# A branch taken out of the last row block, and a sort cut into three pieces between hop products

## The chip, the cores and the metric

One core of one Trainium2 chip runs the kernel. The metric is device microseconds of one execution, as the median of several runs. "PE" is TensorE's matmul, "PEld" its weight load, DVE is VectorE, ACT ScalarE, POOL GpSimd, SP SyncE, which here issues most of the DMAs.

## The reference

Two graph layers over 4096 nodes with 256 features, each as x = x + layer(relu(layernorm(x))). Layer 0 is a graph attention with four heads over the given adjacency. Layer 1 is a diffusion of two steps, and the change lies in it. Cut to what matters:

```python
def _top_p_attention(X, W1, W2, W3):
    q = X @ W1.T @ W2.T
    k = X @ W3.T
    probs = softmax(q @ k.T, axis=-1)
    idx = argsort(-probs, axis=-1)
    sp = take_along_axis(probs, idx, axis=-1)
    cs = cumsum(sp, axis=-1)
    keep_sorted = cs - sp < 0.9          # the fewest largest that reach 0.9
    A = probs * (the mask keep_sorted, put back by idx)
    return A / A.sum(-1, keepdims=True)

R = S + eye(N);  R = R / R.sum(-1, keepdims=True)     # S is the adjacency
for n in range(2):
    A = _top_p_attention(Xa, W1, W2, W3)
    Xf = R @ Xf
    Xa = A @ Xa
    Z = Z + Xf @ U1[n].T + Xa @ U2[n].T
out = layernorm(X + Z) * ln_g + ln_b
```

## The kernel before

The rows are 32 blocks of 128. After layer 0 (until about 822 us) each of the two steps has two stages.

**The hop** is R @ Xf, 4 passes over 8 row blocks each, 32 source blocks in a pass: 128 pairs of a source block and a pass. `hops` is a generator that yields twice in a pair, after each half of its eight products (L577). For pair m an adjacency tile of 512 KB is loaded (`edge`, L547, into four buffers "ar" and one "aru"), in step 1 also a source tile "x" or "xa" of 128 KB (`source`, L537, five buffers); in step 0 the sources lie on the chip. The source is split into a high part (ACT, L554) and a rest (DVE, L555), "hl", five buffers: `split(A, n)`, some four pairs ahead of the products. Where the pair lies on the diagonal (8 pairs in each pass, 80 to 87 in the third), DVE adds the identity to the tile: `own(A, m + 3)`, L564, the "own row". The products of pair m need its tile, its own row and both parts of hl.

**Beside the hop** two more generators are advanced between the halves of the pairs. `fills` makes the projections and the logits of the first three row blocks, their exponentials and first probes. `picks` finds the threshold of these three blocks and masks them, all on DVE: two halves of a probe (L899), `searching`, two halves of the mask (L899). `searching` takes the 8 largest of each of 18 segments (L923, three groups of six, a yield behind each), sorts the 48 largest out of the 144 (L930 and L932, six rounds), yields, and finds the threshold by a running sum (L934 to L941, "the scan group"). In `picks` each yield of `searching` becomes four steps:

```python
            for _ in searching(r, found):
                yield from waits(3)
```

The orders of PE, DVE, ACT, POOL and SP are written out by hand (`manual_schedule`): an instruction stands in its engine's queue where the Python code records it.

**The row blocks** follow, one `attend` for each of the 32: eight groups of four transposes (L1010), ACT's copy of them ("eT", L1012) and eight products (L1018) with the features. `between[g]` puts other work behind group g. For all but the first three blocks the threshold is found here, in `chosen_kept`, by the same `searching` run through at once (`candidates`).

Rows whose 48 candidates don't decide the threshold are counted: `questioned`, `counted`, `chosen`. Blocks with such rows are computed again behind the step: `prepared` makes the exponentials anew, searches by bisection and handles ties (its products are L1134, its exponentials L1139), `completed` redoes the products and writes the rows. In the kernel before, the first such block is prepared inside the last row block, behind its group 0, under a branch on the count that all engines have loaded into a register (L1101):

```python
            def beginning():
                finish(blocks[NB - 2])
                R.count = number(R, R.undone)
                with tc.If(R.count > 0):
                    prepared(R)
```

`finish` adds up block 30's result on DVE. The branch itself, and what each engine does where the body is skipped, have the line L1309. The second branch, in `repaired` (L1178), stands behind the step and holds `completed` and a loop over further blocks. Group 2 of the last block starts hop 2's first loads in step 0 (`begin`: four tiles and four sources), groups 5 and 6 split them; behind the last block PE makes the first halves of hop 2's products.

Of the kernel before, what the change touches and what calls it, by code (L numbers as in the profile page):

```python
# [56 lines left out]
def gat_then_top_p_diffusion(  # L57
# [738 lines left out]
    def table(name):  # L796
        return small.tile([P, NB], F32, name=name, bufs=1)

    def col(name, bufs=None):
        return small.tile([P, 1], F32, name=name, bufs=bufs or 4)  # L800
# [112 lines left out]
    def searching(r, found):  # L913

        t, after, eighth = (x[:, r.b:r.b + 1] for x in found)
        seg = SEG
        cand = small.tile([P, SEG, 8], F32, name="cand", bufs=2)
        best = small.tile([P, CAND], F32, name="best", bufs=2)

        cum = small.tile([P, CAND + 1], F32, name="cum", bufs=2)  # L920
        edges = [N * s // seg for s in range(seg + 1)]
        for s in range(seg):
            nc.vector.max(cand[:, s, :], big[:, edges[s]:edges[s + 1]])  # L923
            if s % 6 == 5:
                yield
        nc.vector.tensor_scalar(cum[:, :1], r.z, 1.0 - TOP_P, r.low3, ALU.mult, ALU.subtract)
        nc.vector.tensor_reduce(eighth, cand[:, :, 7], AX.X, ALU.max)
        flat = cand.rearrange("p s k -> p (s k)")
        for i in range(CAND // 8):
            nc.vector.max(best[:, ts(i, 8)], flat)  # L930
            if i + 1 < CAND // 8:
                nc.vector.match_replace(flat, best[:, ts(i, 8)], flat, -1.0)  # L932
        yield
        nc.vector.tensor_tensor_scan(cum[:, 1:], best, zero.to_broadcast([P, CAND]), cum[:, :1], ALU.add, ALU.add)  # L934

        drop = small.tile([P, CAND], F32, name="drop", bufs=2)
        work = small.tile([P, CAND], F32, name="work", bufs=2)
        nc.vector.tensor_scalar(drop, cum[:, :CAND], 0.0, 3.0e38, ALU.is_ge, ALU.mult)
        nc.vector.tensor_tensor_reduce(work, drop, best, 1.0, best[:, :1], ALU.add, ALU.min, t)
        nc.vector.tensor_scalar(work, drop, -1.0, 3.0e38, ALU.mult, ALU.add)  # L940
        nc.vector.tensor_tensor_reduce(work, best, work, 1.0, -3.0e38, ALU.subtract, ALU.max, after)  # L941
        r.t = t
# [55 lines left out]
    def loads(r):  # L998
        r.xf, r.part = rows.tile([P, KC, P], F32, name="xf"), rows.tile([P, D], F32, name="part", bufs=3)
        nc.sync.dma_start(r.xf, xft_d[r.n][ds(r.b, 1)].rearrange("o p s i -> (o p) s i"))  # L1000
        if r.n > 0:
            nc.sync.dma_start(r.part, block(z_d, r.b))
            r.x1 = rows.tile([P, D], F32, name="x1", bufs=3)
            nc.sync.dma_start(r.x1, block(x1_d, r.b))
        r.acc = ps1.tile([P, 2, D], F32, name="acc")
# [111 lines left out]
    def index(R, engine):  # L1117
        return nc.values_load(R.ids_i[:, :1], engines=[engine], min_val=0, max_val=NB - 1)
# [34 lines left out]
    def completed(R, cur):  # L1153

        r = SimpleNamespace(n=R.n, b=index(R, ET.SP), e=R.e, scale=R.scale)
        dve = index(R, ET.DVE)
        loads(r)
        r.ri = col("a_ri", 1)
        nc.vector.tensor_copy(r.ri, rinv[:, ds(dve, 1)])
        if r.n + 1 < STEPS:  # L1160
            r.x = rows.tile([P, D], F32, name="a_x", tag="xa")
            nc.vector.tensor_copy(r.x, X[:, ds(dve, 1), :].rearrange("p o d -> p (o d)"))
        eT = [turn(r, 0)]
        for g in range(NB // 4):
            if g + 1 < NB // 4:
                eT.append(turn(r, g + 1))
            gather(r, eT[g], g, cur)
        scaled(r)
        contributed(r, contribute(r))
        finish(r)  # L1170
        finish_scale(r)
        finish_rows(r)
        rest = small.tile([1, NB], I32, name="a_rest", bufs=1)
        nc.vector.tensor_copy(rest[:, 1:], R.ids_i[:, 1:])
        nc.vector.tensor_copy(R.ids_i[:, :NB - 1], rest[:, 1:])

    def repaired(R, cur):
        with tc.If(R.count > 0):  # L1178
            completed(R, cur)
            with tc.For_i(0, nc.values_load(R.rest_i, engines=everyone, min_val=0, max_val=NB), 1):  # L1180
                prepared(R)
                completed(R, cur)
# [70 lines left out]
    for n in range(STEPS):  # L1253
        cur = X
        G = SimpleNamespace()
        found = [table(f"found{i}") for i in range(3)]
        blocks = {}
        with tc.manual_schedule(engines=every):
            pieces = first_hop if n == 0 else hops(second)
            filling, picking = fills(n, G, found, blocks), picks(n, found, blocks)  # L1260
            done = 0 if n else NB - G0 - LOOK
            for i, _ in enumerate(pieces, 2 * done):
                if n > 0 and i % 6 == 5 and i // 6 < NB // 4:
                    g = i // 6
                    nc.sync.dma_start(cur[:, ts(g, 4), :], xa_d[ts(g, 4)].rearrange("b p d -> p b d"))
                if (n == 0 or i > 10) and i // 2 % NB != NB - 2:
                    next(filling, None)
                    if i // 2 % NB < NB - 3 or i % (2 * NB) == 2 * NB - 1:
                        next(picking, None)
                if i == 2 * len(order) - 6:  # L1270
                    first = turn(blocks[0], 0)
            weights(n)
            for _ in filling:
                next(picking, None)
            for _ in picking:
                pass

            def chosen_kept(b):

                r = blocks[b]  # L1280
                if not hasattr(r, "kept"):
                    candidates(r, found)
                if b > 2:
                    finish_scale(blocks[b - 3])
                if b + 2 < NB and not hasattr(blocks[b + 2], "stepped"):
                    first_step(blocks[b + 2])
                if b + 1 < NB and not hasattr(blocks[b + 1], "thirded"):
                    third_probe(blocks[b + 1])
                if b > 1:
                    finish(blocks[b - 2])  # L1290
                if b > 2:
                    finish_rows(blocks.pop(b - 3))
                if not hasattr(r, "kept"):
                    masked(r)

            R = SimpleNamespace(n=n, kT=G.kT, qT=G.qT, nm=G.nm, table=found[0])

            def last_chosen():
                chosen_kept(NB - 1)
                R.failed, R.undone = questioned(G, found)  # L1300

            def looked():
                counted(R)
                chosen(R)

            def beginning():
                finish(blocks[NB - 2])
                R.count = number(R, R.undone)
                with tc.If(R.count > 0):  # L1309
                    prepared(R)  # L1310

            beside = {NB - 2: {5: last_chosen, 6: looked}, 0: dict(zip((0, 1, 3, 5, 6), S.turned))}
            for b in range(NB - 1):
                chosen_kept(b)
                if b + AHEAD < NB:
                    blocks[b + AHEAD] = began(n, b + AHEAD, G)
                attend(blocks[b], cur, blocks.get(b - 1), blocks.get(b + AHEAD),
                       beside.get(b, {}), [first] if b == 0 else ())
            r = blocks[NB - 1]

            def earlier():
                for b in range(NB - 3, NB - 1):
                    finish_scale(blocks[b])
                for b in range(NB - 3, NB - 1):
                    finish_rows(blocks[b])

            beside = {0: beginning, 3: earlier}
            if n + 1 < STEPS:
                second = hop_of(n + 1)
                beside.update({2: lambda: begin(second, 4), 5: lambda: split(second, 2), 6: lambda: (split(second, 4), own(second, 4))})  # L1330
            attend(r, cur, blocks[NB - 2], None, beside)
            contributed(r, contribute(r))
            for m in range(second.begun if n + 1 < STEPS else 0):
                for s in range(KC):
                    graph_products(second, m, s, (0,))
            finish(r)
            finish_scale(r)
            finish_rows(r)
        repaired(R, cur)


# [30 lines left out]
```

## Time and profile before

| | |
|---|---|
| median of 3 runs | 2939.87 us (2936.16, 2939.87, 2939.92) |
| profiled execution | 2939.0 us, span 2937.2 us |
| busy: PE, PEld | 2832.3 us (96%), 2476.5 us (84%) |
| busy: DVE, ACT, POOL | 2197.3 us (75%), 1912.0 us (65%), 761.9 us (26%) |
| mean granted TensorE clock | 0.987 |
| products of hop 1 | about 822 to 1137 us |
| row blocks of step 0 | about 1140 to 1881 us |
| products of hop 2 | about 1881 to 2184 us |
| row blocks of step 1 | about 2187 us to the end |

In the timelines a row gives start and length in us, engine, line, operation, what is written and read, the number of instructions, and in brackets the idle time ahead of it on that engine and what ended it. "DVEq" or "PEldq" are rows of an engine's sequencer: branches, register loads, semaphores. A product of 128x512 is shown with 0.39 us, but the next one starts 0.23 us after it; a pair takes 1.83 us.

### The profile page before, as it was taken

The page shows a single profiled execution, that of the slowest core. Times are in us where ns is not written, and L with a number is a line of the kernel's source. Part 1 is how long each engine was busy: PE and PEld are TensorE (multiplying, and loading weights), DVE is VectorE, ACT ScalarE, POOL GpSimd, SP SyncE. Part 2 cuts the span into 40 slices and gives each one's busy share as a digit, 9 for nine tenths or more (in the row PEclk, how much of TensorE's full clock was granted, in tenths as well). Part 3 has the DMA queues.
Part 4 walks back from the last instruction along what each step waited for, and adds up shares of the span by engine and source line. Part 5 has one row for each costly group of instructions (what it writes and reads, how often), then busy time and mean ns, then how long its engine had stood idle before and what let it go on. Part 6 is the DMA issues. An engine that isn't in the chain of part 4 may idle for free. (4 is left out here: it accounts for less than half of the span.)

```text
span 2937.2 us, 51997 instructions
## 1 busy us (share of the span) xinstructions
PE 2832.3 (96%) x19033; PEld 2476.5 (84%) x19033; DVE 2197.3 (75%) x5193; ACT 1912.0 (65%) x3063; POOL 761.9 (26%) x1657
## 2 busy tenths in 40 slices
PE   5799999999999999999999999899999999999997
PEld 3699999999977778888888888788778888888886
DVE  6766877778654383788888888442837999999996
ACT  5776787867733634777777776235337777777772
POOL 5501211112010220222332222000203444444441
PEclk7899999999999999999999999999999999999999
DMA  7969578594455784000000000488970000001000
GB/s 161 199 236 237 169 243 188 221 228 182 177 187 161 241 282 165 20 20 20 25 21 20 20 20 18 152 266 279 334 272 22 25 25 25 25 28 31 25 23 22
DMA packets 181152, 368.16 MB, mean 125 GB/s; under 512 B 17168, under 2 KB 133904, under 8 KB 176784
## 3 DMA queue, kind: packets, MB, share of 16 engines
q1 hardware_dynamic: 142352, 270.92, 28.0%
q0 software_dynamic: 21504, 83.89, 12.0%
q10 hardware_dynamic: 17024, 9.85, 1.1%
q8 instruction: 155, 2.54, 0.4%
q14 instruction: 117, 0.96, 0.1%
HBM read 301.35 MB, written 109.38 MB: 140 GB/s over the span
## 5 line engine op out<-in xcount | busy, mean ns | idle before, releaser
L1018 PE MATMUL acc<-X,eT 128*128 128x256 f32 x4096 | 965.6, 381 | 0.0
L1018 PEld LDWEIGHTS acc<-X,eT 128*128 128x128 f32 x4096 | 743.2, 190 | 97.2 <-ACT eT L1012 14.4
L378 PE MATMUL acc<-ut,m 128*128 128x195 bf16 (+1 forms) x8192 | 700.5, 247 | 5.5 <-DVE st L395 5.5
L378 PEld LDWEIGHTS <-m 128*128 128x128 fp8e4 x8192 | 696.7, 97 | 9.4 <-DVE st L395 4.6
L837 ACT ACTIVATE e<-mm,nm 128x1024 f32<-128x1024 f32 x256 | 286.7, 1120 | 311.1 <-PE mm L677 296.5
L352 ACT ACTIVATE g<-sr,d_big 128x1024 uint8<-128x1024 f32 x444 | 467.5, 1139 | 2.6 <-DVE m L358 2.6
L1012 ACT COPY eT<-tp 128x512 f32<-128x512 f32 x512 | 299.1, 584 | 104.0 <-PE tp L1010 103.1
L905 DVE SCALAR_TENSOR_TENSOR big<-e,c 128x4096 f32<-128x4096 f32 x58 | 273.0, 4706 | 121.4 <-POOL c L890 84.3
L861 POOL TENSOR_TENSOR sums<-sums 128x2 f32<-128x2 f32 x64 | 12.5, 196 | 1310.2 <-ACT void L844 1310.2
L577 PE MATMUL mm<-ar,hl 128*128 128x512 f32 x844 | 337.1, 402 | 12.9 <-issue 5.6
L923 DVE MAX8 cand<-big 128x8 f32<-128x228 f32 (+1 forms) x1152 | 348.3, 380 | 0.0
L577 PE MATMUL acc<-ar,hl 128*128 128x512 f32 x844 | 330.2, 394 | 1.4 <-DVE ar L564 1.4
L1010 PE MATMUL tp<-ident,e 128*128 128x128 f32 x2048 | 310.7, 274 | 7.8 <-DVEq L1309 5.8
L1010 PEld LDWEIGHTS tp<-ident,e 128*128 128x128 f32 x2048 | 248.6, 141 | 77.1 <-ACT eT L1032 27.8
L358 DVE TENSOR_TENSOR m<-g,ax 128x512 uint32<-128x512 uint32 x256 | 182.2, 712 | 116.9 <-PE acc L378 96.9
L947 DVE SCALAR_TENSOR_TENSOR e<-e,found 128x4096 f32<-128x4096 f32 x58 | 259.6, 4476 | 0.0
L844 ACT ACTIVATE void<-e,c1x 128x2048 int8<-128x2048 f32 x128 | 257.4, 2011 | 2.5 <-issue 1.7
L844 ACT ACTIVATE void<-e,c 128x2048 int8<-128x2048 f32 x128 | 257.4, 2011 | 0.0
L577 PEld LDWEIGHTS mm<-ar,hl 128*128 128x128 f32 x844 | 160.1, 190 | 50.8 <-issue 11.7
L677 PE MATMUL mm<-kT,qT 128*128 128x512 f32 x512 | 198.3, 468 | 3.6 <-ACT e L837 2.2
L359 DVE TENSOR_TENSOR m<-m,ax 128x512 uint32<-128x512 uint32 x256 | 177.8, 694 | 26.4 <-DVE m L358 1.4
L577 PEld LDWEIGHTS acc<-ar,hl 128*128 128x128 f32 x844 | 160.2, 190 | 33.8 <-DVE ar L564 1.8
(297 smaller groups left out, 3491.4 us busy)
## 6 DMA issues: line engine op xcount, KB each, us to landing
ar<-adj_d SPq DMA_DIRECT2D x211, 512.0 KB, 4.8
adj_d<-ax POOLq DMA_DIRECT2D x32, 2048.0 KB, 7.3
ut<-uv_d SPq DMA_DIRECT2D x60, 784.0 KB, 5.3
aru<-adj_d SPq DMA_DIRECT2D x45, 512.0 KB, 4.8
ax<-in_adj_t_dram POOLq DMA_DIRECT2D x32, 512.0 KB, 15.8
x<-xf_d SPq DMA_DIRECT2D x78, 128.0 KB, 4.8
xf<-xft_d SPq DMA_DIRECT2D x64, 128.0 KB, 2.2
sr<-s_d SPq DMA_DIRECT2D x15, 512.0 KB, 4.8
```

What stands on the lines that cost most here:

```text
L352: nc.scalar.activation(g[:, c, :], shared[k].sr, AF.Relu, scale=BIG, bias=d_big[:, h, j:j + 1])
L378: nc.tensor.matmul(shared[k].acc[i][:, t, :cols], m[t][:, c, ts(i, P)], shared[k].ut[j // QUARTER][:, j % QUARTER, t, :cols], start=(j == ...
L577: nc.tensor.matmul(A.acc[c][s], A.hl[m][:, t, ts(s, P)], A.ar[m][:, ts(c, 512)], start=(j == 0 and t == 0), stop=(j == NB - 1 and t == 1))
L677: nc.tensor.matmul(pm[:, h, :], q[t], kT[:, ds(h * (N // 2) + c * 512, 512)], start=(t == 0), stop=(t == 1))
L837: nc.scalar.activation(ev[:, :, c, :], r.pm[c], AF.Exp, bias=r.nm, accum_out=r.sums[:, c // 2, c % 2:c % 2 + 1])
L844: nc.scalar.activation(void, r.e[:, ts(h, N // 2)], (AF.Relu, AF.Sign)[i], bias=r.c1, scale=-1.0, accum_out=r.sums[:, h, 2 + i:3 + i])
L905: nc.vector.scalar_tensor_tensor(big, r.e, r.c3, r.e, ALU.is_le, ALU.mult, accum_out=r.low3)
L923: nc.vector.max(cand[:, s, :], big[:, edges[s]:edges[s + 1]])
L947: nc.vector.scalar_tensor_tensor(r.e, r.e, r.t, r.e, ALU.is_ge, ALU.mult, accum_out=kept)
L1010: nc.tensor.transpose(pt[:, i, :], r.e[:, ts(4 * g + i, P)], ident)
L1012: nc.scalar.copy(eT, pt)
L1018: nc.tensor.matmul(r.acc[:, 0, :], eT[:, i, :], cur[:, j, :], start=(j == 0), stop=(j == NB - 1))
```

## The change

The branch in `beginning` goes, the load of the count stays. `prepared` is recorded ahead of `completed` inside the branch of `repaired`, so that the redo of the first block stands behind the step as a whole. In `searching` the yield behind the sort moves into its loop, behind every second round: three pieces of two rounds with a yield each. In `candidates`, which runs the generator through at once, nothing changes.

```diff
@@ searching
             nc.vector.max(best[:, ts(i, 8)], flat)
             if i + 1 < CAND // 8:
                 nc.vector.match_replace(flat, best[:, ts(i, 8)], flat, -1.0)
-        yield
+            if i % 2:
+                yield
@@ repaired
         with tc.If(R.count > 0):
+            prepared(R)
             completed(R, cur)
@@ beginning
                 finish(blocks[NB - 2])
                 R.count = number(R, R.undone)
-                with tc.If(R.count > 0):
-                    prepared(R)
```

In the built programs PE's order differs in the branch alone; on DVE the rows of the picking stand otherwise between the splits. In pairs of the hop, counted by the split ahead of which a row stands:

| rows on DVE | step 0 before | step 0 after | step 1 before | step 1 after |
|---|---|---|---|---|
| block 0: sort | 79 | 79, 80, 82 | 76 | 76, 78, 79 |
| block 0: scan group | 80 | 83 | 78 | 81 |
| block 0: mask halves | 81, 83 | 84, 86 | 79, 80 | 82, 83 |
| block 1: probe halves | 85, 86 | 88, 89 | 82, 84 | 85, 87 |
| block 1: sort | 92 | 95, 97, 101 | 90 | 93, 94, 96 |
| block 1: mask halves | 95, 96 | 103, 105 | 92, 94 | 101, 102 |
| block 2: sort | 108 | 114, 116, 117 | 106 | 112, 113, 115 |
| block 2: mask halves | 111, 112 | 120, 121 | 108, 110 | 117, 119 |

## The prediction

> **What bounds the kernel now.** The page first: PE is busy 2832.3 of 2937.2 us, so only what stops PE counts. Then the timeline around the branch on R.count, and the list for its line, L1309, with the sequencers' own rows. Then the waits of PE in the two hop stages, and the timeline around each sort (L930, L932).
>
> The branch. First the timeline of step 1's last row block, then one line of step 0's, then the list of L1309:
>
> ```profile
> 2906.04 1.89 PE L1018 MATMUL acc<-X,eT 128*128 128x256 f32 x8
> ...
> 2911.11 0.63 PE L1010 MATMUL tp<-ident,e 128*128 128x128 f32 x4 [3.18 <-DVEq L1309]
> ```
> ```profile
> 1863.83 0.63 PE L1010 MATMUL tp<-ident,e 128*128 128x128 f32 x4 [2.66 <-DVEq L1309]
> ```
> ```profile
> L1309 DVEq EVENT_SEMAPHORE  x4: 21/21/21, 1863.7 to 2911.1; - x4
> ...
> L1309 DVEq COMPARE_BRANCH  x2: 68/70/72, 1860.6 to 2908.1; - x2
> ...
>   PE tp L1010: 5.8, 2
> ```
>
> PE ends gather 0 at 2907.93 and stands until 2911.11, although the group it transposes next was masked long before. It waits for a semaphore that VectorE adds up on the far side of the branch: DVE reaches the branch at 2908.1, 70 ns later it is decided, and its next instruction comes 2.8 us after that. PE's own branch is over under gather 0. No row of L1134 or L1139 exists: the body never ran, the count was 0 in both steps.
>
> The sort. Step 0's hop, block 0, from the timeline:
>
> ```profile
> 1035.59 0.43 DVE L555 TENSOR_TENSOR hl<-X,hl 128x256 fp32r<-128x256 f32 x1 [3.62 <-ACT hl L554]
> ...
> 1036.15 0.30 DVE L930 MAX8 best<-cand 128x8 f32<-128x144 f32 x1
> ...
> 1040.12 0.44 DVE L555 TENSOR_TENSOR hl<-X,hl 128x256 fp32r<-128x256 f32 x1
> ...
> 1040.62 0.50 PE L577 MATMUL mm<-aru,hl 128*128 128x512 f32 x1 [2.40 <-DVE hl L555]
> ...
> 1045.01 0.28 DVE L564 TENSOR_TENSOR ar<-ar,ident 128x128 fp32r<-128x128 f32 x1
> 1045.21 2.34 DVE L899 SCALAR_TENSOR_TENSOR e<-e,found 128x2048 f32<-128x2048 f32 x1
> 1045.39 0.47 PE L577 MATMUL mm<-ar,hl 128*128 128x512 f32 x1 [3.11 <-issue]
> ```
>
> The sort holds DVE from 1036.15 to 1040.12, 3.97 us, while PE needs a split row block (hl, L555) every 1.83 us. The second gap is called "issue", but it ends 0.1 us after the own row (L564) of pair 80: here 1 is added to the diagonal of the adjacency tile, and pairs 80 to 87 can't start before it. Step 1's hop, the same place:
>
> ```profile
> 2090.84 0.28 DVE L564 TENSOR_TENSOR ar<-ar,ident 128x128 fp32r<-128x128 f32 x1
> ...
> 2091.22 0.77 PE L577 MATMUL mm<-ar,hl 128*128 128x512 f32 x1 [2.53 <-issue]
> ```
> The windows of both places (PE, PEld, DVE, ACT, POOL busy; clock; DMA share; GB/s):
> ```profile
> 1036.00:1050.00 14.00, 8.49 (x29) 5.97 (x28) 13.48 (x42) 2.84 (x8) 12.31 (x21) 0.88 0.58 184
> ...
> 2120.00:2132.00 12.00, 12.00 (x55) 9.80 (x54) 10.79 (x30) 3.41 (x8) 0.00 (x0) 1.00 1.00 369
> ```
> DVE is the bound around 1036 to 1050, and the clock fell; step 1 elsewhere runs against a full DMA share.
>
> **The branch, part by part.** Removed in each step: five COMPARE_BRANCH and the semaphore rows behind them. The five register loads of the count (0.29 to 0.54 us, in the sequencers) stay; PE's lies at 2904.48, under L1038. Behind gather 0, PE then waits only for its own earlier products and ACT's eT copies (0.58 us in a group of 2.17, each after 1.58 idle). What is late next: nothing on PE; DVE's finish ended at 2907.86 and is wanted again at group 3. SP loses the branch ahead of hop 2's four x and four ar loads, which come some 0.4 us earlier, long before their use. The two q_s loads inside the body go past them into the redo's body and don't run. Gain: 2.66 + 3.18 = 5.84 us, PE's whole waits. Bounds: 0, if another wait ends at the same time, and 5.84; I take 5.84, as the order names no other.
>
> The redo's branch at the step's end (L1178) now jumps over a longer body. Today DVE needs 2.9 us there, PE 3.3 to 3.8, under the last products or beside SP's wait for the z_d store; ACT and SP need 0.4. Cost 0 if ACT and SP stay so; the other bound is a rival below.
>
> **The sort, part by part.** The rows stay: per block six MAX8 and five replaces, 3.97 us. Added are two yields per sort, each four halves of a hop pair in the picking: six halves, three pairs, per block, 18 halves by the third. Only the first three blocks of a step are picked so. The order shows the third ending at split 123 (step 0) and 248 - 128 = 120 (step 1) of 128, so nothing is left bare behind the hop. No DMA and no work of ACT, PE or POOL changes its place. The new waits are DVE's: a piece may stand behind a split whose ACT cast isn't there, and behind it stand the mask halves (L899) and own rows, for which PE waits.
>
> I add DVE's rows up in the new order: a split 0.34, two rounds 1.50 (the last piece 1.08), the scan group 1.24, a half with its read 2.28, own 0.28, six MAX8 of L923 1.87.
>
> Step 0: split 78 starts at 1035.59 as now. Split 79 at 36.15 + 1.50 = 37.65 (now 40.12): the 2.40 shrinks to 0.1. Splits 80, 81 at 39.49 and 39.83, the last piece to 41.25, split 82, own 80 done at 41.87: PE, ready at 39.55, starts pair 80 at 1041.97 (now 1045.39). Then the scan and four halves lie among own rows: PE waits 1.0 at pair 82 and 0.85 at pair 87, and reaches pair 88 at 1058.45 instead of 1061.77: 3.3 us. Today's ten pairs take 26.0 us against 18.3 undisturbed, so the loss is 7.7 and 4.4 of it stay: the own rows are then the bound.
>
> Step 1: split 75 ends at 2076.02 as now. With pieces, splits 76 to 79 come at 2077.7, 2078.2 (its cast), 2080.05 and 2081.5, split 80 at 2083.05 (its x load, issued at 2077.43, isn't earlier), then the scan group, split 81, a half, and split 82 at 2087.3, own 80 at 2087.9, before PE needs it (2088.47). The 2.53 goes, and so does the half clock behind it; new waits of 0.5 and 0.2 come at pairs 81 and 86. Pair 88 at 2103.85 instead of 2107.26: 3.4 us. (Today's ten pairs take 22.4 against 18.3, a loss of 4.1.) The gap at 2139.19 (2.5 us) stays: SP issued nothing between 2130.42 and 2134.85, its L547 load being held, and no sort is near that.
>
> Bounds of the two: 7.7 and 4.1 if all loss goes; 0 and 0 if it only moves; below nothing if the half masks pile up among the own rows (a rival). I take the sums, since the same addition over today's order is the measured row itself.
>
> The clock: gaps of 3.11 and 2.53 (and 2.35 at 1891.69) were followed by some 3.4 us in which matmuls came every 0.43 instead of 0.23 us; those of 2.40, 2.51 and 3.18 were not. In step 0 this lay mostly under the wait for own 81, so it costs 0.7 there, and some 1.2 in step 1. The Trainium skill, "TensorE: Matmul & The Clock Gate" (section "Why this matters for your kernels"), has the clock fall only over gaps of some 3 us; by that the step-1 term would be 2.2, and the sum 1.2 us smaller. The trace differs with 2.53 and 2.35 us, and it decides.
>
> **Sum.** 5.84 + 3.3 + 3.4 = 12.5. The profiled execution took 2939.0 us (span 2937.2 and 1.8 around it), giving 2926.5; the median of the three runs, 2939.87, gives 2927.4. I say 2927.0.
>
> **Rivals.**
> Branch only: the picks' gaps move but don't shrink. For it: DVE is busy 13.48 of 14 us, and no row is removed. Against: PE's lead over own 80 recovers by 2.5 to 3.4 us in both sums. 2939.0 - 5.8 = 2933.2. Chance 0.17.
> All loss goes: own rows cost less than summed. 5.84 + 7.7 + 4.1 = 17.6: 2921.4. Chance 0.12.
> DMA holds step 1: share 1.00 to 1.06 at 369 to 392 GB/s between 2070 and 2132, and PE would ask for as much without a pause; step 1's 3.4 is lost: 2929.9. Against: 345 GB/s at share 0.96 feeds 2142 to 2184 with only 0.26 us of gaps. Chance 0.12.
> The jumps: ACT's or SP's jump over the longer body costs DVE's 2.9 us instead of 0.4. On SP that ends at 1885.8 instead of 1883.4; its waits end at 1884.9 today, so hop 2's loads come 1.4 later, and the kernel's end 1.2 later: 12.5 - 2.6, 2929.1. The Trainium skill, "Runtime: NRT & Kernel Launch" (section "Instruction fetch mechanics"), says that a taken branch stalls where its target lies outside the two pages being held; DVE's 2.8 against ACT's 0.4 agrees, and by it any engine can fall on the wrong side. Chance 0.05.
> Slower: DVE without lead at the diagonal. Place: pairs 80 to 91 of each hop, where halves, MAX8 and own rows now make 21.4 us of DVE work against 18.2 of PE in ten pairs of step 1. If DVE comes there late, a hop loses the 3.2, three pairs of lookahead (5.5) and three half-clock stretches of 1.7: 13.8, twice 27.6, against today's 11.8; with the branch gone 2939.0 + 15.8 - 5.8 = 2949. It decides when own 80 is done over 5.5 us behind PE's need; my sums have it 2.4 late and 0.6 early. Chance 0.06.
>
> **How the numbers follow.** The forecast has 0.48. A change under 0.2% (5.9 us, about what a measurement of this kernel can tell; the runs before spread by 3.8) is no change. Faster, below 2934.0: 0.48 + 0.12 + 0.12 + 0.05, and 0.07 of branch-only, which lies 0.8 inside the line: 0.84. Same: its other 0.10. Slower: 0.06. The range leaves out the slower rival and the outer half of all-loss: 2920 to 2936.
>
> **What would show it.** No gap behind gather 0 in either last block (if one stays, the branch term is wrong). Step 0: no wait near 2.4 before split 79, pair 80 near 1042 and waits of 1 us among the own rows; if PE reaches pair 88 at 1061 or later, the sums fail. Step 1: own 80 before PE needs it, no half clock there; if PE waits for ar loads instead, DMA it was. The gap behind SP's hold stays. At the ends, ACT's and SP's jumps at 0.4 us. A time over 2936 would make the forecast wrong.

## The result, and the profile after

The changed kernel takes 2928.58 us (median of 7 runs, 2922.21 to 2930.05) against 2939.13 us of the kernel before (7 runs): ratio 0.9962, 95% interval 0.9952 to 0.9971, so 11.2 us faster, 8.5 to 14.1. The forecast was 2927.0, some 12 us faster. The profiled execution took 2926.2 us (span 2924.4; before 2937.2).

PE's busy time hardly moves (2828.4 us against 2832.3): the gain is idle time. The two groups of PE that the change aimed at, from the costliest groups (behind the second bar: idle time ahead of the group and what ended most of it):

```profile
L577 PE MATMUL mm<-ar,hl 128*128 128x512 f32 x844 | 335.1, 400 | 13.8 <-DMA ar<-adj_d 5.8
...
L1011 PE MATMUL tp<-ident,e 128*128 128x128 f32 x2048 | 310.6, 274 | 2.2
```

Lines are one higher than before here. The transposes (L1011) had 7.8 us of idle ahead of them, 5.8 of it put down to the branch; 2.2 are left. The hop's products (L577) had 12.9 us, the largest part (5.6) "issue"; they now have 13.8, the largest part (5.8) the adjacency tiles' DMA. So the branch's gaps went and the hop's waits changed their releaser. The timeline of PE in step 1's last row block, and in step 0's hop (ACT and POOL left out):

```profile
2896.92 1.89 PE L1019 MATMUL acc<-X,eT 128*128 128x256 f32 x8
2898.65 0.60 PE L1011 MATMUL tp<-ident,e 128*128 128x128 f32 x4
2899.09 1.89 PE L1019 MATMUL acc<-X,eT 128*128 128x256 f32 x8
```
```profile
1033.77 0.43 DVE L555 TENSOR_TENSOR hl<-X,hl 128x256 fp32r<-128x256 f32 x1 [3.62 <-ACT hl L554]
...
1039.38 0.28 DVE L564 TENSOR_TENSOR ar<-ar,ident 128x128 fp32r<-128x128 f32 x1
...
1039.76 0.47 PE L577 MATMUL mm<-ar,hl 128*128 128x512 f32 x1 [1.92 <-issue]
...
1044.37 0.47 PE L577 MATMUL mm<-ar,hl 128*128 128x512 f32 x1 [0.69 <-ACT hl L554]
```

The transposes behind gather 0 start 0.16 us before the gather's last row ends. In step 0's hop split 79 no longer keeps PE 2.40 us, and pair 80 starts 0.1 us after its own row (1039.38 + 0.28): the own row is still what PE waits for, as forecast. In step 1 the waits between pairs 68 and 90 are these:

```profile
2068.12 0.47 PE L577 MATMUL mm<-ar,hl 128*128 128x512 f32 x1 [0.96 <-ACT void L844]
2075.14 0.47 PE L577 MATMUL mm<-ar,hl 128*128 128x512 f32 x1 [1.16 <-DMA ar<-adj_d]
2085.28 0.47 PE L577 MATMUL mm<-ar,hl 128*128 128x512 f32 x1 [0.72 <-issue]
```

The 2.53 us and the half clock behind it are gone, but an adjacency tile came late twice ("ACT void" names an engine that was long done; the tile landed at 2067.99).

Between the two profiled executions the 12.7 us of span arise so: 2.5 ahead of the change's place (1.5 of it a stretch at half clock at 923 us, in hop 1, which of these two only the execution before had), 3.5 at step 0's sort, 2.85 in its last row block, 1.3 lost at hop 2's start, 1.5 at step 1's sort, 3.4 in the last row block, 0.3 at the end. Two executions can't tell which of these belong to the change; twelve more can.

### The profile page after: what moved, and what is told of

It is laid out like the page before. It is cut to its first block, busy times and chain, and to the rows that moved or that the text cites. A ratio compares the mean times of both kernels' runs of the same rounds, so it can differ in the third digit from the quotient of the medians.

```text
span 2924.4 us, 51961 instructions
## 1 busy us (share of the span) xinstructions
PE 2828.4 (97%) x19033; PEld 2473.4 (85%) x19033; DVE 2196.4 (75%) x5193; ACT 1913.3 (65%) x3063; POOL 759.9 (26%) x1657
## 5 line engine op out<-in xcount | busy, mean ns | idle before, releaser
L1019 PEld LDWEIGHTS acc<-X,eT 128*128 128x128 f32 x4096 | 743.2, 190 | 97.4 <-ACT eT L1013 14.6
L577 PE MATMUL mm<-ar,hl 128*128 128x512 f32 x844 | 335.1, 400 | 13.8 <-DMA ar<-adj_d 5.8
L577 PE MATMUL acc<-ar,hl 128*128 128x512 f32 x844 | 328.1, 392 | 1.5 <-DVE ar L564 1.4
L1011 PE MATMUL tp<-ident,e 128*128 128x128 f32 x2048 | 310.6, 274 | 2.2
L1011 PEld LDWEIGHTS tp<-ident,e 128*128 128x128 f32 x2048 | 248.9, 141 | 70.5 <-ACT eT L1033 27.9
L577 PEld LDWEIGHTS mm<-ar,hl 128*128 128x128 f32 x844 | 158.9, 188 | 52.0 <-issue 12.8
L577 PEld LDWEIGHTS acc<-ar,hl 128*128 128x128 f32 x844 | 158.9, 188 | 33.7 <-DVE ar L564 2.3
```

Of the source, the lines that this page charges most:

```text
L577: nc.tensor.matmul(A.acc[c][s], A.hl[m][:, t, ts(s, P)], A.ar[m][:, ts(c, 512)], start=(j == 0 and t == 0), stop=(j == NB - 1 and t == 1))
L1011: nc.tensor.transpose(pt[:, i, :], r.e[:, ts(4 * g + i, P)], ident)
L1019: nc.tensor.matmul(r.acc[:, 0, :], eT[:, i, :], cur[:, j, :], start=(j == 0), stop=(j == NB - 1))
```

## The experiments

Every kernel was timed against the kernel before on its own chip, and profiled once. Ratios are to the kernel before. Two stretches of the hops are compared throughout, from the starts of pairs' first products: pairs 76 to 88 of step 0 and 68 to 88 of step 1. Undisturbed, at 1.83 us a pair, they would take 22.0 and 36.6 us.

**Each part alone, and the changed kernel again.** `e1_branch_only` is the kernel before with the branch part of the diff, `e2_sort_only` with the sort part, `e3_after_again` the changed kernel.

> Only the branch is taken out, the sort stays in one piece. My theory (two independent parts): the gaps of PE behind gather 0 of both last row blocks go, 2.66 and 3.18 us in the profile of before and some 0.2 us more each because the transposes then run under the tail of the gather: 5.8 to 6.2 us, so 2932.9 to 2933.3 us against 2939.1 of before. The gaps at L577 in the hops stay as before: near 2.4 and 3.1 us in step 0, near 2.5 us in step 1. Rival, the parts are not independent (the sort's gain was partly luck of the clock, and the branch part brought the rest): some 8 to 11 us, or 2928 to 2931 us.

> Only the sort is in pieces, the branch stays. My theory: 3.3 to 3.5 us in step 0 (pair 80 by 1.5 to 3.5 us earlier) and 1.5 to 3.4 us in step 1, so 4.8 to 6.9 us: 2932.2 to 2934.3 us. The waits for L1309 of 2.7 and 3.2 us stay. Rival, the gaps only move (branch only): 2939 us, with pair 88 of each hop where it was in before, measured from pair 76.

> The changed kernel once more, to see in a second profile what varies between executions. Theory: about 2928.6 us; pairs 76 to 88 of step 0's hop gain again 3.3 to 3.6 us against before, the two branch gaps are absent again, and the DMA waits of 1.0 and 1.2 us at pairs 70 to 76 of step 1's hop are there again if they belong to the schedule. Rival, they are chance of one execution: then step 1's gain from pair 68 to pair 88 is near 3 us here instead of 1.5.

Measured, against 2941.31: 2930.89 (0.9962, 0.9948 to 0.9975) for the branch alone; 2935.11 (0.9980, 0.9971 to 0.9989) for the sort alone; 2925.94 (0.9943, 0.9930 to 0.9957) for both. Both parts gain, and their sum (16.6 us) is about what both together give (15.4). But the branch alone gives 10 us where the traces' gaps held 6. In the first's own trace the last row blocks, from their first product to their last, gained 2.85 and 3.36 us, as expected. The sort alone shows where more can come from. PE in its last row block of step 1:

```profile
2906.05 1.09 PE L1011 MATMUL tp<-ident,e 128*128 128x128 f32 x4 [3.20 <-DVEq L1310]
2906.93 3.62 PE L1019 MATMUL acc<-X,eT 128*128 128x256 f32 x8
2910.34 1.06 PE L1011 MATMUL tp<-ident,e 128*128 128x128 f32 x4
```

Here the branch's gap (3.20 us, in the kernel before 3.18) was followed by 6.8 us at half clock: eight products in 3.62 us instead of 1.89. The last row blocks of step 0 and 1 took 20.7 and 22.6 us; in the kernel before 19.1 and 19.6; without the branch 16.2 in each. So the branch cost 6.2 us in one execution and 10.8 in another.

In `e3` the tiles of step 1 came late again (waits of 1.53 and 0.76 us up to pair 76), and pairs 68 to 88 took 41.8 us: these waits are no chance of one execution.

**Is it the jump or the join?** `e4_small_body` is the changed kernel with the sort whole and a branch in the old place around a body of one instruction:

```diff
                 R.count = number(R, R.undone)
+                with tc.If(R.count > 0):
+                    nc.vector.tensor_copy(R.t, zero)
```

> Sort in one piece as in before, and the body joined to the redo, but a branch on R.count is kept in its old place around a body of one small VectorE copy (not executed, as the count is 0). It tells the jump from the join. Theory, the length of VectorE's jump: the branch is decided in 0.1 us, its next instruction follows in some 0.1 to 0.5 us, and PE's wait behind gather 0 falls from 2.7 and 3.2 us to 0.8 or less: 4 to 6 us gained, 2933 to 2935 us. Rival, the join of the engines at the branch itself, whatever the body: waits of 2.5 to 3.2 us stay, 2939 us. Third, the place of the target and not the length decides: the two steps may differ, one with a wait near 3 us and one without, 2936 us.

Measured: 2930.96 us (0.9963, 0.9950 to 0.9977), the time of the kernel without any branch. The list of its branch line:

```profile
L1310 DVEq COMPARE_BRANCH  x2: 72/72/72, 1861.6 to 2903.9; - x2
L1310 DVEq EVENT_SEMAPHORE  x2: 21/21/21, 1861.8 to 2904.1; - x2
```

DVE's next instruction comes 0.2 us behind the branch instead of 2.8 to 3.0, and PE waits no more: both last row blocks take 16.2 us, as without the branch. Neither the branch, nor the count's load, nor the meeting of the engines cost PE anything: the jump over the long body did. That settles the cause of the gap. Whether length or place of the target decides, this run can't tell, since a body of one instruction is short wherever it lies.

**What does the half clock behind the branch cost?** `e5_before_filled` and `e10_before_filled22` are the kernel before with 12 and 22 extra transposes (result unused) on PE ahead of the branch:

```diff
                 finish(blocks[NB - 2])
+                pt = ps2.tile([P, 4, P], F32, name="tp")
+                for i in range(22):
+                    nc.tensor.transpose(pt[:, i % 4, :], blocks[NB - 1].e[:, ts(i, P)], ident)
                 R.count = number(R, R.undone)
```

> Before, with twelve extra transposes (about 1.3 us of PE, result unused) queued behind gather 0 of the last row block and ahead of the branch. They lie inside the gap, so the gap itself stays: 2.7 and 3.2 us from gather 0's end to the next useful transpose. Theory (the clock): in six profiles every window of 3.41 us on a fixed grid in which PE idled 57% or more was followed by a window at half clock, and none with 56% or less; before's branch gaps lay at 55 and 56% in the profiled run, and at 71 and 70% in the run with only the sort changed, where they cost 1.6 and 3.0 us more. The filler takes the idle time to 1.4 and 1.9 us, under 57%. So it is faster than before by what the half clock costs in the mean of runs, 2 to 4.5 us: 2936.8 to 2939.3 us against 2941.3. Rival, the wait alone counts and the clock behind it is nothing: no change, or 0 to 1 us slower.

> As the run with twelve extra transposes behind gather 0 of before, but with 22 (about 2.4 us), so that PE idles only some 0.3 and 0.8 us at the branch instead of 1.4 and 1.9. The gap to the next useful transpose stays. Theory (clock): no window at the branch can reach 57% idle, so no half clock follows in any run; faster than before by 3 to 4.5 us. The twelve gave 1.3 us by medians (interval 0 to 5), with a window at 55%. Rival: the clock behind the branch is not what made the kernel without the branch 10 us faster instead of 6; then no more than 1 us.

Measured: 2938.24 against 2939.53 (0.9992, 0.9983 to 1.0001) and 2936.20 against 2938.33 (0.9994, 0.9986 to 1.0003). PE at the branch of step 1 with 22:

```profile
2899.86 1.89 PE L1018 MATMUL acc<-X,eT 128*128 128x256 f32 x8
2901.58 2.56 PE L1310 MATMUL tp<-ident,e 128*128 128x128 f32 x22
2904.94 0.63 PE L1010 MATMUL tp<-ident,e 128*128 128x128 f32 x4 [0.79 <-DVEq L1312]
```

The filler lies in the gap and costs nothing, and no half clock followed in either profile. Point values of 2.4 and 1.8 us less would fit a clock loss in part of the executions, but both intervals reach no change, and the 3 to 4.5 us that I expected of the second aren't borne out. That the clock accounts for all the branch gave beyond 6.2 us is not shown. The intervals leave room for it: 7.3 us is the low end for the branch alone.

**Where did step 1's sort gain go?** `e8_pieces_step0` cuts the sort in step 0 alone; `e7_stores_later` is the changed kernel with the stores of the drained passes 22 pairs later in step 1:

```diff
-            if i % 2:
+            if i % 2 and r.n == 0 or i + 1 == CAND // 8:
                 yield
```
```diff
-                    if turned and j > 2 and j % 2:
+                    if turned and j > (24 if A.hop else 2) and j % 2:
                         turned.pop(0)()
```

> The changed kernel with the sort in pieces in step 0 alone; step 1's sort is whole as in before. My prediction gave 3.4 us to step 1's sort: by it this is 3.4 us slower than the changed kernel, some 2931 us. Theory now: step 1's hop took 301.4, 301.1 and 302.9 us with pieces and 301.5, 300.1 and 299.2 with the sort whole, so nothing is lost: the time of the changed kernel within 1.5 us, 2926 to 2929 us.

> The changed kernel with the stores of the drained pass (four of 256 KB, L593) issued in step 1's hop 22 pairs later (pairs 57, 89, 121 instead of 35, 67, 99); step 0 unchanged. Theory (transfers took the gain of the sort in step 1): pairs 68 to 88 of step 1 took 40.0 to 42.2 us in six profiles, the same with the sort whole or in pieces, since 1 MB of stores lands among the adjacency tiles there; without them they take 38.5 to 39.5 us, and the gap at pair 104 where SP's load waits behind those stores (1.9 + 0.6 us) goes too. Time 2 to 4 us under that of the changed kernel. Rival: the stores are not what the tiles wait for, and pairs 68 to 88 stay at 40 to 42 us; then only the gap at pair 104 moves: within 1 us.

With the sort whole in step 1: 2925.74 us (0.9952, 0.9938 to 0.9965), no slower than the changed kernel's 0.9962 and 0.9943. So cutting step 1's sort gave nothing that the times show; their intervals alone don't rule out 3.4 us. The stretches of the profiles that bear on it:

| us | sort whole | mean | sort in pieces | mean |
|---|---|---|---|---|
| step 0, 76 to 88 | 29.7 (before), 31.5, 30.4, 30.5, 30.0 (e1, e4, e5, e10) | 30.4 | 26.2 (after), 26.8, 25.6, 26.9, 26.3, 25.7 (e2, e3, e7, e8, e9) | 26.3 |
| step 1, 68 to 88 | 42.2 (before), 40.4, 40.0, 40.2, 40.7, 40.0 (e1, e4, e5, e8, e10) | 40.6 | 40.7 (after), 41.4, 41.8, 41.1 (e2, e3, e6) | 41.3 |

Left out are `e6` in step 0 (34.1, own rows on another engine) and, in step 1, `e7` and `e9` (37.3 and 40.9, stores elsewhere), `e11` and `e12` (39.6 and 39.1, another start of the hop). The execution from which I forecast had the longest step-1 stretch of all, by its 2.53 us gap and the half clock behind it. In the other five with the sort whole, what PE waited for rows and splits at pairs 80 to 83 was 0.6 to 1.4 us, without half clock. The longest of these waits, in `e1`:

```profile
2087.14 0.47 PE L577 MATMUL mm<-ar,hl 128*128 128x512 f32 x1 [1.36 <-issue]
```

With the sort in pieces these waits are 0.5 to 0.9 us, while those for tiles are 1.9 to 2.7 instead of 1.2 to 1.8 (2.3 and 1.4 in the mean); the whole increase lies at pairs 76 to 78. With the stores away from there, in `e7`, pairs 68 to 88 took 37.3 us, and PE waited for no tile. From that kernel's timeline, its only wait between 2060 and 2090, and its windows (PE, PEld, DVE, ACT, POOL busy; clock; DMA share; GB/s):

```profile
2085.83 0.47 PE L577 MATMUL mm<-ar,hl 128*128 128x512 f32 x1 [0.27 <-issue]
```
```profile
2070.00:2090.00 20.00, 19.73 (x86) 15.73 (x86) 16.38 (x46) 4.65 (x13) 6.59 (x17) 1.00 1.01 363
```

So with the 1 MB of stores there, PE waits longer for tiles when DVE stops it less. Little of the forecast gain was there in the mean of executions, and these waits took it back. (How long pairs 68 to 88 take with the sort whole and the stores away was not run.) The full DMA share alone didn't make PE wait: this window moved 363 GB/s at a share of 1.01 without a wait for a tile. What did is seen in SP's timeline in the changed kernel, ahead of the wait of 1.16 us at 2075.14:

```profile
2066.59 0.38 SPq L537 DMA_DIRECT2D xa<-xf_d  x1
2069.69 0.32 SPq L547 DMA_DIRECT2D ar<-adj_d  x1
```

SP issued nothing for 2.72 us, and the late tile was asked for 0.06 us after the last of ACT's four stores had landed (2069.63). Every wait of over 0.25 us for a tile at pairs 76 to 78, in seven profiles, has this hold of SP ahead of it (2.3 to 3.3 us), and so has the gap at pair 104 wherever the stores are at pair 99. Ahead of the late tiles of pair 73 no store had just landed, and their cause is open. Nor does the trace show why SP waits for a store of ACT's.

But pairs 88 to 96, where the stores of the second pass now lie, took 17.7 us instead of 14.7: 3.1 given back, 2.7 of it in one wait behind the same hold. In time it is 2926.73 us (0.9954, 0.9940 to 0.9968), no measurable change. `e9_stores_spread` issues them one at a time:

```diff
+            if hop and not last:
+                return [lambda i=i: stored((i,)) for i in range(2 * KC)]
             return [stored] + (...
-                    if turned and j > 2 and j % 2:
+                    if turned and j > 2 and (j % 7 == 3 if A.hop else j % 2):
```

> The changed kernel with the four 256 KB stores of a drained pass in step 1's hop issued one by one, at the fourth, 11th, 18th and 25th pair of the next pass, instead of all at the fourth. Theory (transfers took the sort's gain in step 1): moved by 22 pairs, the stores left pairs 68 to 88 at 37.3 us instead of 40.7 and 41.8, but pairs 88 to 104 took 32.4 instead of 31.3 and 31.6; one at a time each finds slack, as 512 KB of adjacency and 128 KB of rows per pair of 1.83 us are 358 GB/s and the windows of before moved up to 392. So pairs 68 to 88 take 37.5 to 38.5 us, 88 to 127 stay near 75.4, step 1's hop takes 298 to 299 instead of 301.4 to 302.9, and the time is 2 to 4 us under the changed kernel's, 2923 to 2926 us. Rival: the sum of bytes counts and not when they come; the hop stays at 301 to 303 us and the waits are spread.

2932.67 us (0.9975, 0.9965 to 0.9985): by the ratios 4 to 9 us slower than the changed kernel. Pairs 68 to 80 took 22.3 us instead of 25.1 and 26.1, but from there on each store brought a wait. Three of them, 10 to 14 us behind the stores at 2086.14, 2102.13 and 2140.31:

```profile
2099.62 0.47 PE L577 MATMUL mm<-ar,hl 128*128 128x512 f32 x1 [1.02 <-DMA ar<-adj_d]
...
2112.05 0.47 PE L577 MATMUL mm<-aru,hl 128*128 128x512 f32 x1 [1.12 <-DMA aru<-adj_d]
...
2152.59 0.47 PE L577 MATMUL mm<-ar,hl 128*128 128x512 f32 x1 [1.34 <-DMA ar<-adj_d]
```

The hop took 309.0 us instead of 301 to 303. My theory of slack was wrong, and the rival too mild: four stores issued apart cost more than four together. The trace has the reason: behind each of the seven stores from 2057.15 to 2155.46 SP issued nothing for 2.7 to 7.1 us, and its next load went out 0.06 to 0.07 us after the store had landed. For the four of the second pass that is 21.4 us in sum, against 5.1 with the four together in the changed kernel.

**Do own rows bind in step 0?** `e6_own_on_pool` puts them on GpSimd; `e11_own_early_fill_late` records them one pair earlier in step 0, and, far from there, starts hop 2's projections two pairs later:

```diff
-                    nc.vector.tensor_tensor(block_, block_.bitcast(F32), ident, ALU.add)
+                    nc.gpsimd.tensor_tensor(block_, block_.bitcast(F32), ident, ALU.add)
```
```diff
-                own(A, m + 3)
+                own(A, m + (3 if A.hop else 4))
@@
-                if (n == 0 or i > 10) and i // 2 % NB != NB - 2:
+                if (n == 0 or i > 14) and i // 2 % NB != NB - 2:
```

> The changed kernel with the own rows (L564, 1 added to the diagonal of the adjacency tile) on GpSimd instead of VectorE. My prediction said that 4.4 us of step 0's loss stay because own rows stand behind the sort's pieces and half masks in VectorE's queue. Theory: with a queue of their own PE's gaps at pairs 80 to 88 of step 0 (1.9 + 0.4 + 0.7 us in the profile of after) fall to 0.5 us or less in sum, pairs 76 to 88 of step 0 take 23.5 to 24.5 us instead of 25.6 to 26.8, and the time falls by 2 to 4 us, to about 2924 us. Rival, the split row blocks bind and not the own rows: less than 0.5 us. Other side: GpSimd's addition is slow or stands behind the search steps of GpSimd, and PE waits for it: 2 to 10 us slower.

> The changed kernel with two edits in different places. First, own rows of step 0 come one pair earlier in VectorE's queue (step 1 as it was). Theory of my prediction: own rows bind after the sort, so the gaps of 1.9, 0.4 and 0.7 us at pairs 80 to 88 fall by half or more and pairs 76 to 88 of step 0 take 23.5 to 25 us instead of 25.6 to 26.8. Rival: the sort's pieces and half masks bind through the split row blocks, and it stays within 0.5 us; other side: VectorE waits for the adjacency tile's load, and it is slower. Second, the first projections of hop 2 start four halves (two pairs) later, so that PE doesn't reach the X reload before it has landed (gap of 2.6 to 3.0 us at L708, followed by a stretch at half clock in 9 of 10 profiles). Theory: pairs 0 to 8 of hop 2 without that gap and half clock, 2 to 3 us gained up to pair 16; rival: the transfers are behind there anyway, and the waits go to the adjacency tiles, gain under 1 us.

On GpSimd: 2926.84 us (0.9959, 0.9945 to 0.9973), the changed kernel's time. Its profiled run (2931.79, the slowest of five) shows why the edit is no cure. PE's timeline, then POOL's:

```profile
1043.80 0.80 PE L577 MATMUL mm<-ar,hl 128*128 128x512 f32 x1 [7.93 <-POOL ar L564]
```
```profile
1038.73 2.66 POOL L884 TENSOR_SCALAR up<-up,c1x,yy 128x1 f32<-128x1 f32 x1
...
1043.29 1.69 POOL L564 TENSOR_TENSOR ar<-ar,ident 128x128 fp32r<-128x128 f32 x4
```

The own rows stood behind the 22 small operations of a search step, 11.7 us long, and PE waited 7.93 us: the expectation's other side. The own row's place in a queue matters, but this queue was worse.

One pair earlier on DVE: 2919.15 us (0.9927, 0.9914 to 0.9939), by the ratios 5 to 10 us faster than the changed kernel. Pairs 76 to 88 of step 0 took 23.4 us instead of 26.3. Its PE waits there:

```profile
1039.09 0.47 PE L577 MATMUL mm<-ar,hl 128*128 128x512 f32 x1 [0.52 <-ACT hl L554]
1045.20 0.47 PE L577 MATMUL mm<-ar,hl 128*128 128x512 f32 x1 [0.39 <-issue]
```

So own rows did bind. The second edit took pairs 0 to 8 of hop 2 from 25.5 us to 19.8: PE no longer runs into the X reload (2.65 us in the changed kernel). Part comes back when the delayed work is due, at pairs 48 to 64 (40.5 us instead of 35.9); the hop as a whole took 297.5 us against 301.4 and 302.9.

**A combination.** `e12_combined` adds to that kernel the later stores for the third pass alone:

```diff
-                    if turned and j > 2 and j % 2:
+                    if turned and j > (24 if A.hop and p == PASSES - 1 else 2) and j % 2:
```

> The kernel with own rows one pair earlier in step 0 and hop 2's projections two pairs later, and in addition the stores of the third drained pass of step 1's hop at pair 121 instead of 99 (those of the first two passes stay at pairs 35 and 67). Theory: the gap at pair 104 is SP's load held behind ScalarE's four stores, and at pair 121 hardly any load is left to be held; pairs 96 to 104 take 14.7 us as in the kernel with all stores later, instead of 16.7 to 17.3, and 104 to 127 some 43 to 43.5; so 2 to 3.5 us under the 2919.2 us of the kernel without that edit: 2915.7 to 2917.2. Rival: the bytes of the stores cost the same wherever they are issued, as they did when spread; then the waits move to pairs 121 to 127 and it stays at 2918 to 2921 us.

Measured: 2915.91 us (0.9927, 0.9913 to 0.9940, against 2937.86), the fastest here by its median, although its ratio is that of `e11`. Pairs 96 to 104 took 14.6 us instead of 16.7 to 17.3, as the theory had it: SP's load is no longer held there. Hop 2 took 292.4 us, and no half clock occurred between 250 us and the last products.

## Why the prediction was right, and where it wasn't

**The branch's gap: right.** PE waited for DVE's jump and for nothing else. 5.84 us was forecast; free of the clock it is 6.2 (2.86 + 3.37), since the transposes now also overlap the gather's tail. `e4` shows the jump as the cause. One wait behind it was put at nothing: hop 2 comes earlier and waits for its loads. Its pairs 0 to 8 took 23.9 to 24.6 us in the four profiles with the branch's gap and 23.7 to 25.9 in the eight without it that start hop 2 alike; the means are 24.3 and 25.0, so some 0.7 us went back, though the two overlap.

**The branch's clock: the step that was missing.** I priced the half clock behind the sort's gaps but not behind the branch's two, because the profile of before showed none there. By the windows below, its two gaps filled 55 and 56% of one, a share that only some of the windows pay for. In `e2` they filled 71 and 70% and cost 4.6 us more. How often they do is not settled: the filler runs put the mean at 2 us, with 0 inside their intervals.

**The sort in step 0: right, a little small.** 3.3 forecast, 4.1 in the mean (30.4 to 26.3). The addition of DVE's rows had pair 88 at 1058.45; shifted by the 2.50 that were ahead of it, it came at 1058.31. So close a match is partly luck, as the single waits fell otherwise: the sums had 1.0 at pair 82 and 0.85 at pair 87, the trace has 0.40 at pair 78, 0.69 at pair 82 and none at pair 87. That 4.4 us would stay was right as well (26.3 - 22.0 = 4.3), and `e11` shows the reason that was given, own rows: in `e11` and `e12` the stretch is 23.4 and 24.1, so 2.2 to 2.9 of it was theirs.

**The sort in step 1: wrong.** The failed term is "3.4 us" for pair 88; it is nothing (40.6 whole, 41.3 in pieces; `e8`). It failed twice. "Today" was one unlucky execution, 1.6 us over the mean of six: its 2.53 us was 0.6 to 1.4 in the other five. And the next wait was put at nothing: the waits for tiles grew from 1.4 to 2.3 us. So the rival "DMA holds step 1" had this term's outcome, but not its cause, which was SP's hold behind ACT's stores for the waits at pairs 76 to 78, and not the full DMA share. Its "against", 345 GB/s with 0.26 us of gaps between 2142 and 2184, came from a stretch without stores.

**What stays, and the jumps.** The gap behind SP's hold stayed (1.9 us at pair 104), and `e12` shows the reason: SP's load waits behind ACT's stores, and with them elsewhere the gap is gone. The longer body did change a jump: ACT's, in step 0.

```profile
L1179 ACTq EVENT_SEMAPHORE  x4: 17/17/17, 1873.6 to 2915.2; - x4
...
L1179 ACTq COMPARE_BRANCH  x2: 50/54/58, 1871.0 to 2914.6; - x2
```

2.6 us in step 0, 0.5 in step 1; before, 0.4 in both. ACT had nothing due, so it cost nothing; SP's jump stayed at 0.4 to 0.5. The Trainium skill, "Runtime: NRT & Kernel Launch" (section "Instruction fetch mechanics"), has a taken branch stall where its target lies outside the two pages held, so by it the place of the target decides. ACT's jump over a body of the same code, short in one step and long in the other, agrees.

**The other rivals.** "Branch only" and "all loss goes" are both ruled out by step 0, where 4.1 went and 4.3 stayed. DVE never lost its lead at the diagonal: in step 0 pair 80's own row kept PE 1.9 us, far from the 5.5 at which that rival decides.

**The number.** 6.2 + 4.1 - 0.7 = 9.6 by the profiles' means, and the measured 11.2 (8.5 to 14.1) holds it. With the 0.7 lost at hop 2's start it is 8.9, still inside. The total came out right in part by luck: the term for step 1, which was nothing, was offset by a step 0 larger by 0.8 and a branch larger by 0.4, and by some 2 us that no run assigns; the clock behind the branch may be among them, which isn't shown.

## What to carry to other kernels

An idle gap's price is its length plus the clock behind it, and the second is drawn anew in each execution: take a gap's cost from several profiles, and look for the clock even where the one at hand shows none. Before crediting a gap in a stage whose DMAs run at their full share, ask what the engine will wait for once it isn't stopped, and look at windows that hold the stage's stores too: a store that one engine issues may hold back another engine's loads. A branch whose body never runs can still cost the jump over it; an instruction that others wait for is moved ahead in its own queue before it is moved to another engine's.

## What the runs showed of the hardware

**The clock counts idle time in fixed windows.** The granted clock changes only on a grid of 3.413 us, whose phase differs from run to run. With PE's idle time in the 14 profiles put into that grid (windows at full clock from 250 us to the last row block's end, idle at least 38%): of 90 windows with 38 to 52% idle none was followed by half clock, of 15 with 53 to 56% seven were, of 29 with 57% or more all 29. So some 1.95 us of idle in one window were always enough, in one gap or several (1.17 and 0.98 us in `e2`); a gap of 2.4 us costs half a window of clock or nothing, depending on where the grid falls. The sharp limit between 56 and 57% in the expectation of `e5` doesn't hold: in before itself half clock followed a window that was 55.5% idle, at 919.9 us. The Trainium skill, "TensorE: Matmul & The Clock Gate" (section "What's actually happening"), has the free-running window of 3413 ns, and the grid agrees; its advice against gaps over some 3 us (section "Why this matters for your kernels") is too lax here.

**GpSimd beside VectorE.** In `e6` POOL's L884, 128x1, took 2.66 us where it ran beside DVE's mask half (L899, 2.35 us from 1038.98), and 0.34 to 0.42 elsewhere. All seven operations of the search steps over 1.2 us, in the profiles of after and `e6`, lie beside a probe or mask half (L899). The Trainium skill, "Trainium Architecture — The Big Picture" (section "What this means for kernel authors"), says that the two engines share a port under an exclusive lock, which agrees.

**A load behind another engine's stores.** In each of the 14 profiles a load of SP in hop 2 went out 0.05 to 0.08 us after a 256 KB store of ACT's had landed, and SP had issued nothing for 3.5 to 7.1 us before it (in the kernel before until 2134.85, with the store landed at 2134.80).
